# A fused two-block kernel: more of the state space scan beside the expert layers, less beside the attention

## The chip, the cores and the metric

The kernel runs on one core of one Trainium2 chip. The metric is the time of one execution in microseconds (us). The engines of the core are named as in the profile: PE is TensorE (matrix products; PEld its weight loads), DVE is VectorE, ACT is ScalarE, POOL is GpSimd, SP is SyncE. Each engine works through its own list of instructions in order; all five lists run side by side, and an instruction waits until the data and buffers that it needs are ready.

## The reference, cut to what matters

Two blocks follow each other on 8 sequences of 512 tokens with 128 features, all in float32. Each block computes `x = x + s * silu(f)` from the same normalised input.

```
block 0:  s = mamba(xn) -> rms norm -> MLP -> rms norm
          f = two-layer mixture of experts: 24 experts, top 2, four groups of tokens, at most 86 rows
              per expert and group: layer 1 (128 -> 512), layer norm + relu, layer 2 (512 -> 128)
block 1:  s = causal attention, 8 heads of 128
          f = mixture of 128 experts, top 2, at most 32 rows each
mamba:    h[t] = dA[t] * h[t-1] + dBx[t];  y[t] = sum over 16 states of h[t] * C[t]
```

The recurrence runs over 512 tokens, for 256 channels and 16 states, in each of the 8 sequences. The mamba branch and the mixture of block 0 do not depend on each other until the end of the block. The attention of block 1 works sequence by sequence, so it can begin with sequence 0 while the scan still works on the later ones.

## The kernel before, in words

The scan is cut into 64 **steps**. One step handles two of the 16 states of one sequence, so a sequence has 8 steps, and the sequences follow each other; step number n belongs to sequence n // 8, at place k = n % 8. A generator, `model()`, yields after each step, and `step()` runs it one step further. What a step issues (`scan`, L588 to L628):

- ACT issues two DMAs of 512 KB that broadcast two rows of B (`bb`) and of C (`cb`) over the partitions.
- For each half of the channels: ACT makes two tiles `da` (L601); DVE multiplies `bb` into `u` (L603), runs two scans on it (L605) and multiplies `cb` into it (L606). DVE thus does 8 instructions in a step.
- PE transposes `u` and sums it over the states into the bank `py` with 16 matrix products (L627).

Besides the scan, certain places k carry other work of the branch. At k = 0 the sequence before is gated (L647), `py` is opened anew (L616), and the first part of `back` runs (L667 to L678); at k = 1 and k = 2 its second and third parts (L655 to L701, the MLP). At k = 4 and k = 5 the two parts of `front` of the next sequence run (convolution L559, projection L564, then the step size L576 to L584). At k = 6 the gate is computed (L639).

The buffers of the scan are few: two each of `bb`, `cb` and `da`, four of `u`, one of `py`.

The rest of the kernel is written in a fixed order, and the steps are put between its parts by counting. The stages are:

1. Preparation and routing of the 24-expert mixture, then `step()` once.
2. **First layer**: a loop over the 24 experts (`expert1`: POOL gathers token rows, PE transposes and multiplies, ACT scales, SP stores to DRAM).
3. **Joining stage** (`between`): 16 pairs of token tiles are gathered, layer-normalised on DVE and ACT, and stored.
4. **Second layer**: a loop over the 24 experts (`expert2`: gather, four transposes, four products per tile, and so on).
5. **Turn** to block 1: the mixture's result of sequence 0 is gathered and the attention prepared, with 4 steps placed between.
6. **Attention**: 48 heads (8 of each of the sequences 0 to 5), and after each head the share of the steps that are left. Each head's instructions are `probabilities` (L846 to L860) and `values` (L874 to L892); the copy at L876 may go to DVE or ACT.
7. **Last stage**: the last two sequences' heads beside the 128-expert mixture and the output.

A generator `mixture()` runs the stages 2 to 4 and says, after each expert or pair, how many steps that stage should have in all and in how many parts; the caller adds the shares up and calls `step()` whenever more than half a step is due:

```
    for n, of in mixture():
        due += n / of
        while due > 0.5:
            step()
            due -= 1.0
```

The attention takes what is left: `left = NSTEP - taken`, spread evenly over the 48 heads. Place in the code gives priority: the framework that builds the kernel orders each engine's list by it, and lets a later instruction go first where an earlier one would not be ready. So a step need not run exactly where the code has it.

Of the kernel before, what the change touches and what calls it, by code (L numbers as in the profile page):

```python
# [27 lines left out]
E0, C0, DH, H0 = 24, 86, 512, 4  # L28
# [19 lines left out]
def tile_kernel(ctx: ExitStack, tc: tile.TileContext, t: dict, out: bass.AP):  # L48
# [373 lines left out]
    def weights(shape, source):  # L422

        tiles = {}

        def get(e):
            for n in range(e, min(e + 3, E0)):
                if n not in tiles:
                    tiles[n] = me.tile(list(shape), F32, name="we", tag="we", bufs=4)
                    Q.dma_start(tiles[n], source[n])  # L430
            return tiles[e]

        return get

    def expert1(e, w):

        we = w(e)
        px = ps_e.tile([P, SLOTS], F32, name="px", tag="pe")
        for c, r in enumerate(SROWS):
            xg = me.tile([CP, D], F32, name="xg", bufs=8)  # L440
            gather(xg[:r], xn_dram, inv[:r, c, e : e + 1])
            T.transpose(px[:, c * CP : c * CP + r], xg[:r], ident[:r, :r])  # L442
        xT = me.tile([P, SLOTS], F32, name="xTe", tag="xTe")
        S.copy(xT, px)
        hs = me.tile([CP, SG, DH], F32, name="hs", tag="big", bufs=4)
        for c, r in enumerate(SROWS):
            ph = ps_e.tile([CP, DH], F32, name="ph", tag="pe")
            T.matmul(ph[:r], chosen(e, r), bias[:, 0:DH], start=True, stop=False)
            T.matmul(ph[:r], xT[:, c * CP : c * CP + r], we, start=False, stop=True)  # L449
            S.activation(hs[:r, c, :], ph[:r], AF.Copy, scale=wsl[:r, c, e : e + 1])  # L450
        store(hs_dram, e, hs)
# [52 lines left out]
    def expert2(e, w):  # L504
        we = w(e)
        po = ps_e.tile([CP, SG, D], F32, name="po", tag="pe")
        os = me.tile([CP, SG, D], F32, name="os", tag="o")
        hg = me.tile([CP, SG, DH], F32, name="hg", tag="big", bufs=4)
        for c, r in enumerate(SROWS):
            gather(hg[:r, c, :], hid_dram, inv[:r, c, e : e + 1])  # L510
            pt = ps_e.tile([P, NJ, CP], F32, name="pht", tag="pe")
            for f in range(NJ):
                T.transpose(pt[:, f, :r], hg[:r, c, f * P : (f + 1) * P], ident[:r, :r])  # L513
            hT = me.tile([P, NJ, CP], F32, name="hgT", tag="xTe")
            S.activation(hT[:, :, :r], pt[:, :, :r], AF.Relu)  # L515
            T.matmul(po[:r, c, :], chosen(e, r), bias[:, DH:], start=True, stop=False)
            for f in range(NJ):
                T.matmul(po[:r, c, :], hT[:, f, :r], we[:, f, :], start=False, stop=(f == NJ - 1))  # L518
            S.activation(os[:r, c, :], po[:r, c, :], AF.Copy, scale=wsl[:r, c, e : e + 1])
        store(os_dram, e, os)  # L520
# [526 lines left out]
    def mixture():  # L1047
        w = weights((P, DH), t["W1"])
        for e in range(E0):
            expert1(e, w)  # L1050
            yield 11, E0
        w = weights((P, NJ, D), t["W2"])
        w(0)
        for _ in between():
            yield 6, NTT // 2
        for e in range(E0):
            expert2(e, w)
            yield 14, E0

    step()  # L1060
    due = 0.0
# [5 lines that stand above are left out]
# [155 lines left out]
```

## Time and profile before

| | us |
|---|---|
| median of 8 runs | 1605.14 |
| lowest, highest run | 1598.34, 1609.62 |
| time of the profiled execution | 1606.63 |
| its span, first to last instruction | 1604.9 |

| engine | busy us | share of the span |
|---|---|---|
| PE | 1230.3 | 77% |
| DVE | 1244.0 | 78% |
| ACT | 977.4 | 61% |
| POOL | 599.6 | 37% |

The profile is of one execution. Busy time is the union of an engine's instructions; a window view cuts the span into stretches and gives it for each. In the views, `u<-da,u` means an instruction that writes tile `u` and reads `da` and `u`; `x256` is a count; "idle before" is the time in which the engine stood still just ahead of the instructions of a group, with what ended most of it. The median of the runs and the profiled execution differ by 1.5 us.

### The profile page before, as it was taken

What the parts mean: (1) busy time and instruction counts of PE and PEld (TensorE: products, weight loads), DVE (VectorE), ACT (ScalarE), POOL (GpSimd) and SP (SyncE); (2) the same over time, 40 slices, a digit from 0 to 9 for tenths busy, and PEclk for the clock granted to TensorE, in tenths of its full rate; (3) what the DMA queues carried; (4) which work ended last, traced back from release to release, by engine and by line L of the source; (5) the groups of instructions that cost most, each with busy time, mean ns of one, the idle gap of its engine ahead of it and who ended that gap; (6) DMA issues with size and microseconds to landing.
All of it is one profiled execution on the core that took longest, in us unless ns stands there. A gap on an engine that the chain in (4) does not pass through costs nothing.

```text
span 1604.9 us, 20658 instructions
## 1 busy us (share of the span) xinstructions
PE 1230.3 (77%) x6825; PEld 865.8 (54%) x6825; DVE 1244.0 (78%) x2758; ACT 977.4 (61%) x1727; POOL 599.6 (37%) x502
## 2 busy tenths in 40 slices
PE   6778889513379888646889889989889898899763
PEld 4444355313267777523556656766557576567542
DVE  5628775788946858868999999999899996465454
ACT  6035858666747677445776858676587674642452
POOL 1235643556245434473603550043150402010465
PEclk9678989756679999767989999999999999999886
DMA  6267767787467765533222332123122210548143
GB/s 190 77 219 233 250 235 229 228 253 252 165 191 232 236 181 190 146 72 105 62 72 86 79 96 77 53 87 91 59 66 64 82 44 14 139 117 225 50 112 95
DMA packets 170669, 218.84 MB, mean 136 GB/s; under 512 B 16618, under 2 KB 118074, under 8 KB 170562
## 3 DMA queue, kind: packets, MB, share of 16 engines
q1 hardware_dynamic: 126018, 99.39, 20.1%
q10 hardware_dynamic: 18432, 67.12, 12.8%
q0 software_dynamic: 26112, 51.01, 12.2%
q8 instruction: 54, 0.88, 0.2%
q14 instruction: 53, 0.43, 0.1%
HBM read 161.56 MB, written 55.84 MB: 135 GB/s over the span
## 4 chain that ended last, share of the span: by engine, by line
DVE 37%; PE 30%; issue 9%; DMA 8%; POOL 7%; ACT 7%; another core or an unknown queue 2%; SPq 1%; POOLq 0%; DVEq 0%; ACTq 0%
DVE u L605 11%; DVE u L606 5%; PE po L881 4%; PE sc L854 3%; DVE u L603 3%; DVE sc L856 3%; POOL o L131 3%; PE py L627 3%; PE ph L449 2%; PE pp L874 2%; PE po L518 2%; DVE s L892 2%; POOL hd L128 2%; PE pqm L846 2%
## 5 line engine op out<-in xcount | busy, mean ns | idle before, releaser
L605 DVE TENSOR_TENSOR_SCAN u<-da,u 128x512 f32<-128x512 f32 x256 | 312.8, 1243 | 62.8 <-ACT da L601 54.6
L627 PE MATMUL py<-ident,u 128*128 128x128 f32 x1024 | 165.3, 303 | 135.3 <-DVE u L606 135.2
L627 PEld LDWEIGHTS py<-ident,u 128*128 128x128 f32 x1024 | 133.3, 157 | 187.9 <-DVE u L606 169.5
L881 PE MATMUL po<-v,pT 128*128 128x129 f32 x1280 | 185.6, 288 | 29.4 <-DVE pT L876 13.6
L881 PEld LDWEIGHTS po<-v,pT 128*128 128x128 f32 x1280 | 167.6, 200 | 59.8 <-issue 25.0
L601 ACT ACTIVATE da<-dt,a_neg 128x512 f32<-128x512 f32 x256 | 176.2, 718 | 36.1 <-DVE u L605 30.0
L860 ACT ACTIVATE prob<-sc,mn 128x128 f32<-128x128 f32 (+3 forms) x256 | 130.0, 527 | 102.3 <-DVE mn L856 81.2
L854 PE MATMUL sc<-xaT,qm 128*128 128x128 f32 (+3 forms) x512 | 179.5, 460 | 16.7 <-ACT prob L860 14.2
L603 DVE TENSOR_TENSOR u<-bb,lp 128x1024 f32<-128x1024 f32 x128 | 154.8, 1230 | 14.1 <-DMA bb<-xd_dram 11.7
L606 DVE TENSOR_TENSOR u<-u,cb 128x1024 f32<-128x1024 f32 x128 | 157.9, 1233 | 1.2 <-DMA cb<-xd_dram 0.2
L856 DVE CUSTOM_DVE_ANT_0 sc<-sc,mask 128x128 f32<-128x128 f32 (+3 forms) x256 | 124.8, 499 | 39.8 <-PE sc L854 19.9
L131 POOL DMA_INDIRECT o<-os_dram,row x64 | 113.9, 1780 | 79.4 <-DMA bb<-xd_dram 31.7
L874 PE MATMUL pp<-ident,prob 128*128 128x128 f32 x640 | 113.5, 287 | 37.0 <-DVE pT L876 22.5
L128 POOL DMA_INDIRECT xg<-xn_dram,inv x72 | 93.0, 1292 | 120.9 <-PE px L442 59.9
L828 POOL DMA_INDIRECT xs_dram<-xn,idx x64 | 76.4, 1194 | 161.9 <-DVE row L825 73.3
L874 PEld LDWEIGHTS pp<-ident,prob 128*128 128x128 f32 x640 | 80.7, 147 | 96.7 <-issue 32.6
L128 POOL DMA_INDIRECT hg<-hid_dram,inv x72 | 90.8, 1261 | 101.1 <-PE pht L513 72.0
L854 PEld LDWEIGHTS sc<-xaT,qm 128*128 128x128 f32 x512 | 83.6, 197 | 59.9 <-ACT prob L860 30.5
L128 POOL DMA_INDIRECT hd<-hs_dram,row x64 | 82.0, 1281 | 65.3 <-ACT xs L560 23.4
L876 ACT COPY pT<-pp 128x384 f32<-128x384 f32 (+1 forms) x100 | 51.4, 514 | 63.1 <-PE pp L874 60.6
L518 PEld LDWEIGHTS po<-we,hgT 128*128 128x128 f32 (+1 forms) x576 | 71.8, 189 | 23.0 <-issue 18.4
L518 PE MATMUL po<-we,hgT 128*128 128x128 f32 (+1 forms) x576 | 80.5, 287 | 0.9 <-ACT hgT L515 0.8
(289 smaller groups left out, 2567.4 us busy)
## 6 DMA issues: line engine op xcount, KB each, us to landing
bb<-xd_dram ACTq DMA_DIRECT2D x64, 512.0 KB
cb<-xd_dram ACTq DMA_DIRECT2D x64, 512.0 KB
we<-in_W SPq DMA_DIRECT2D x48, 256.0 KB
hs_dram<-hs SPq DMA_DIRECT2D x24, 512.0 KB
hid_dram<-hd SPq DMA_DIRECT2D x32, 256.0 KB
we<-in_we SPq DMA_DIRECT2D x16, 512.0 KB
hs_dram<-hs SPq DMA_DIRECT2D x24, 192.0 KB
xb<-in_x SPq DMA_DIRECT2D x16, 256.0 KB
```

The source lines that it names most:

```text
L128: G.indirect_dma_start(dst, None, table[:, :], IOA(idx, 0))
L131: G.indirect_dma_start(dst, None, table[:, :], IOA(idx, 0), compute_op=ALU.add)
L518: T.matmul(po[:r, c, :], hT[:, f, :r], we[:, f, :], start=False, stop=(f == NJ - 1))
L601: S.activation(da[:, j, :], dt[:, hf, :], AF.Exp, scale=a_neg[:, hf, n0 + j : n0 + j + 1])
L603: V.tensor_tensor(u, bb, bc(dx[:, hf : hf + 1, :], (P, NC, L)), ALU.mult)
L605: V.tensor_tensor_scan(u[:, j, :], da[:, j, :], u[:, j, :], 0.0, ALU.mult, ALU.add)
L606: V.tensor_tensor(u, u, cb, ALU.mult)
L627: T.matmul(py[:, i, hf * P : (hf + 1) * P], us[hf][:, j, i * P : (i + 1) * P], ident, is_transpose=True, start=False, stop=(n0 + j == DS - ...
L854: T.matmul(sc[:, :w], qm[:, i * P : w], xaT[:, :w], start=True, stop=True)
L856: V.tensor_tensor_reduce(sc[:, :w], sc[:, :w], mask[:, L - w :], -1.0, FMAX, ALU.add, ALU.min, mn[:, i : i + 1])
L874: T.transpose(pp[:, c, :], prob[i][:, k * P : (k + 1) * P], ident)
L881: T.matmul(po[:, i - i0, :], pT[:, i * (i + 1) // 2 + k, :], v[:, k, hd % 4, :], start=(k == 0), stop=(k == i),)
```

## The change

Two numbers in `mixture()` are changed. Between the experts of the first layer there are 14 steps instead of 11, and between those of the second layer 20 instead of 14. The joining stage keeps 6 and the turn 4. Since the attention takes what is left, 19 steps instead of 28 are spread over its 48 heads. No instruction is added or removed.

```diff
         for e in range(E0):
             expert1(e, w)
-            yield 11, E0
+            yield 14, E0
         w = weights((P, NJ, D), t["W2"])
         w(0)
         for _ in between():
             yield 6, NTT // 2
         for e in range(E0):
             expert2(e, w)
-            yield 14, E0
+            yield 20, E0
```

By the code, the steps of each stage are then:

| stage | steps before | steps after |
|---|---|---|
| before the first layer | 0 | 0 |
| first layer | 1 to 11 | 1 to 14 |
| joining stage | 12 to 17 | 15 to 20 |
| second layer | 18 to 31 | 21 to 40 |
| turn | 32 to 35 | 41 to 44 |
| attention | 36 to 63 | 45 to 63 |

## The prediction

> **What bounds the kernel now.** I first cut the span into its stages. The ends are read from the first and last instructions of the tiles (the gathers `xg`, `hd`, `hg`, `o`). In the window view each row is a stretch, its length, then busy time of PE, PE's loads, DVE, ACT and POOL (counts in brackets), granted clock of PE, DMA share, GB/s.
>
> ```profile
> 95.00:290.00 195.00, 155.65 (x614) 83.39 (x613) 135.88 (x127) 125.02 (x205) 94.95 (x75) 0.93 0.73 240
> 290.00:448.00 158.00, 53.05 (x238) 41.02 (x237) 134.49 (x225) 104.66 (x181) 82.93 (x67) 0.63 0.71 224
> 448.00:660.00 212.00, 179.49 (x1309) 152.28 (x1309) 142.83 (x135) 144.22 (x277) 92.27 (x75) 0.95 0.65 199
> 660.00:753.00 93.00, 48.99 (x217) 34.05 (x215) 72.95 (x141) 41.80 (x76) 53.73 (x33) 0.67 0.40 104
> 753.00:1345.00 592.00, 528.53 (x2896) 368.62 (x2896) 568.78 (x1418) 413.95 (x713) 181.78 (x132) 0.96 0.25 71
> ...
> 480.00:640.00 160.00, 141.79 (x1070) 118.63 (x1069) 117.20 (x110) 120.51 (x227) 74.12 (x57) 0.99 0.69 214
> ```
>
> The rows are first layer, joining stage, second layer, turn, attention, and the inner part of the second layer. In the attention DVE is busy 568.8 of 592 us, 96%, and PE 89%: DVE sets its length. In the two layers PE leads: 80% in the first, 85% in the second and 89% (141.8 of 160) in its inner part, with DVE at 70% and 67%. So the change takes work from a stage where DVE is full and puts it where DVE has room and PE has little.
>
> Second, the costliest groups give the price of a step.
>
> ```profile
> L605 DVE TENSOR_TENSOR_SCAN u<-da,u 128x512 f32<-128x512 f32 x256 | 312.8, 1243 | 62.8 <-ACT da L601 54.6
> L627 PE MATMUL py<-ident,u 128*128 128x128 f32 x1024 | 165.3, 303 | 135.3 <-DVE u L606 135.2
> L603 DVE TENSOR_TENSOR u<-bb,lp 128x1024 f32<-128x1024 f32 x128 | 154.8, 1230 | 14.1 <-DMA bb<-xd_dram 11.7
> L606 DVE TENSOR_TENSOR u<-u,cb 128x1024 f32<-128x1024 f32 x128 | 157.9, 1233 | 1.2 <-DMA cb<-xd_dram 0.2
> ```
>
> DVE needs (312.8 + 154.8 + 157.9) / 64 = 9.8 us for a step, PE 165.3 / 64 = 2.6 us. Each group's idle time shows the chain: PE waits for `u`, DVE for `da`.
>
> Third, the waits in the inner part of the second layer.
>
> ```profile
> POOL hg L128 <- PE pht L513: 64.4, 16, 7.7
> ACT os L519 <- PE po L518: 28.7, 20, 4.2
> ...
> PE py L627 <- DVE u L606: 12.1, 13, 1.9
> ...
> DVE u L605 <- ACT da L601: 9.9, 6, 4.0
> ...
> DVE u L603 <- DMA bb<-xd_dram: 7.6, 5, 2.8
> ```
>
> POOL and ACT wait for PE, so PE paces the experts; but of PE's 18 us idle, 12.1 are waits for a step's `u` in PE's in-order list.
>
> **The change part by part.** No instruction comes or goes; 9 steps change their neighbours. Which steps they are matters, since places k differ. The prices per sequence, from the group rows (busy time of the whole kernel over 8), on PE: k = 0 opens `py` 21.5 / 8 = 2.7 and does `pyz` and `pr` (9.1 + 19.4) / 8 = 3.6; k = 1 `pzt`, `pf`, `pr` (7.9 + 36.6 + 33.8) / 8 = 9.8; k = 4 `pc` and `pd` (66.6 + 17.1) / 8 = 10.4; k = 5 `pv` 2.3; k = 6 `pz` 2.3. On DVE: k = 0 1.9 (L647, L678); k = 1 1.5 and k = 2 2.2 (eight short ones of L659, L657, L699); k = 4 0.7 (L566); k = 5 7.3 (four of L582 at 1.22, L583, L584).
>
> *First layer*, three steps more (12, 13, 14; k = 4, 5, 6): PE 3 x 2.6 + 10.4 + 2.3 + 2.3 = 22.8; DVE 3 x 9.8 + 0.7 + 7.3 = 37.4.
> *Joining stage*, still six, but places 5 and 6 give way to 2 and 3: PE -4.6, DVE 2.2 - 7.3 = -5.1. DVE is busy 85% there; I take -3.
> *Second layer*, 21 to 40 for 18 to 31: six scans, two more of k = 0, one more each of k = 1, 5 and 6: PE 15.6 + 12.6 + 9.8 + 4.6 = 42.6; DVE 58.8 + 3.8 + 1.5 + 7.3 = 71.4.
> *Turn*, k = 1 to 4 for 0 to 3: PE +4.1, DVE -1.2. PE is 53% busy there and covers it; without that cover it would be 4. I take +3.
> *Attention*, without 36 to 44: PE 9 x 2.6 + 2 x 10.4 + 2.3 + 2.3 + 6.3 + 9.8 = 64.9; DVE 9 x 9.8 + 2 x 0.7 + 7.3 + 1.9 + 1.5 + 2.2 = 102.5.
>
> These are sums of records that overlap by some 5% on an engine (in the attention the branch's share and the rest add to more than the 568.8 of the union), so the attention is left with about DVE 569 - 98 = 471 and PE 529 - 61 = 468. **Both engines are then equal**, where DVE was ahead. The length has bounds: at the 96% that DVE reaches now, 471 / 0.96 = 491; at the 89% that PE has now, 468 / 0.89 = 526. I take 512 (about 92% of either), nearer the second since two full engines in step lose more than one: gain 592 - 512 = 80, bounds 66 and 101.
>
> In the layers the added PE work is the least that can be charged if PE had no room, 21 and 40 us after the overlap; the idle 39 and 32 us of PE could take half of it; the most is the whole DVE time one for one, 37 and 71, if the step's chain sets the pace. I take the added PE time at the present share of PE: 21 / 0.85 = 25 (0.85 is between 80% and the 84% of its inner part) and 40 / 0.89 = 45. DVE is then (136 + 36) / 220 = 78% and (143 + 68) / 257 = 82% busy, below the 85% of the joining stage, so it can just follow.
>
> Each moved step also brings its ACT work (four `da` of 0.72 us, 2.9 us, plus its table loads of 1.28 us) and two 512 KB DMAs to queues where an expert's scalings stand. ACT goes from 144 of 212 to about 186 of 257 us, 72%, as in the attention (70%): no term. The DMAs take 3.1 us of all 16 engines per MB (19.7% of 212 us for 13.5 MB); the six steps add 19 us to 138 us busy, but the stage grows too, so the share stays near 0.65: no term. Should the `bb` wait double, that is 8 us, inside the range.
>
> Sum: -80 + 25 + 45 - 3 + 3 = -10 us on the profiled 1606.6. I take a little more, -14: in the rows above the granted clock rises with PE's share (0.63 at 34%, 0.93 at 80%, 0.95 at 85%, 0.99 at 89%), so a denser first layer may come from 0.93 to 0.95, which is 2% of 178 us, 4 us. That gives 1592.6; the median of the runs stands 1.5 us below the profiled time, so 1592 holds for either.
>
> [...] The gathers of the layers last longest beside the scan: `xg` issues take 909 / 966 / 2003 ns (least, median, most), `ya` in the last stage, with no step near, 940 / 944 / 1337. Both layers have 72 gathers with a mean of 1.29 and 1.26 us, so some 0.33 us x 144 = 47 us of POOL are lost now; with DVE 8 to 15 points busier than its present 67 to 70%, some 8 more. POOL idles over 95 us in each layer and waits for PE, so the sum has no term for it. [...]
>
> **The rivals.**
> *Slower: the step's chain sets the pace of the layers.* In the layers DVE has nothing but the scan (all its records there are of the branch), so each wait for `da` (ACT's list stands behind scalings that wait for PE) is lost, and PE then waits for `u`. For it: 26.8 us of waits for `da` in the first layer, and 12.1 of PE for `u`. Then the layers grow by DVE's time, 36 + 68 = 104, and the gain is 80: +24, 1630. It decides once DVE passes about 85% in the second layer. Against it: DVE has nearly no wait in the attention at 96%.
> *No change:* PE stays at 89% in the attention (gain 66) and the layers cost 66 to 70: 1605 to 1610.
> *More gain:* idle time of PE in the layers takes half of what comes, +33, and the attention reaches 96%, -101, or 92%, -80: -47 to -68, 1540 to 1560.
>
> **How the numbers follow.** Forecast (1575 to 1600) 0.38; more gain 0.12; no change 0.10; slower 0.40, as the second layer would have to hold 82% of DVE with a chain that now idles a third of its time. A measurement of this kernel tells about 0.3%, 5 us. Faster 0.50, same 0.10, slower 0.40. The range for 8 in 10 runs from 1562 (part of "more gain") to 1634 (the slower rival with a little over); the likeliest case alone has 1575 to 1600.
>
> **What the next profile would show.** If right: the second layer is 250 to 262 us long, the first 215 to 225, PE's share about 0.85 in both; the attention about 512 us with DVE and PE within 3 points of each other. If the slower rival holds: a second layer over 275 us with DVE over PE and longer waits of DVE for `da` and PE for `u`. If the attention is still over 530 us, my equal-engines figure is wrong; if the layers grow by under 40 us together, PE had room that the busy time hides.

## The result: 4% slower, and the profile after

The changed kernel takes 1671.65 us (median of 16 runs), the kernel before 1605.05 us in the runs beside it (46 runs): ratio 1.040, 95% interval 1.038 to 1.042. The medians differ by 67 us. The profiled execution has a span of 1661.7 us against 1604.9, so 57 us are to be found in the profile.

First the window view of the kernel after, by the same stages as before: first layer, joining stage, second layer, turn, attention, last stage, and then the inner part of the second layer. The columns are the length of the stretch, busy time of PE, PE's loads, DVE, ACT and POOL, granted clock, DMA share, GB/s.

```profile
95.00:314.00 219.00, 170.88 (x665) 90.97 (x663) 157.95 (x146) 139.28 (x222) 93.41 (x75) 0.92 0.68 223
314.00:480.00 166.00, 72.70 (x296) 52.68 (x296) 146.26 (x241) 105.17 (x194) 81.26 (x65) 0.64 0.71 228
480.00:747.00 267.00, 208.96 (x1472) 174.72 (x1472) 203.56 (x194) 175.02 (x326) 93.68 (x77) 0.92 0.59 181
747.00:852.00 105.00, 56.03 (x217) 34.53 (x217) 75.48 (x144) 52.39 (x85) 58.47 (x37) 0.67 0.37 94
852.00:1406.00 554.00, 482.01 (x2619) 340.00 (x2617) 475.39 (x1321) 366.15 (x633) 162.76 (x123) 0.95 0.21 57
1406.00:1661.70 255.70, 194.12 (x1164) 137.10 (x1162) 136.74 (x466) 111.32 (x207) 82.61 (x85) 0.88 0.43 118
500.00:735.00 235.00, 185.64 (x1307) 153.36 (x1306) 179.07 (x173) 158.57 (x296) 78.70 (x62) 0.93 0.59 181
```

The attention lost 38 us (592 to 554), where 80 was forecast. DVE and PE are nearly equal in it, 475 and 482 us, as the prediction said (471 and 468), but each is busy for only 86% and 87% of it. The second layer grew by 55 us, from 212 to 267, and PE's share in it fell from 85% to 78%. The first layer grew by 24, the joining stage by 8 and the turn by 12 in these cuts.

In both layers DVE's idle time hardly changed: 195 - 135.9 = 59 us and 219 - 158.0 = 61 in the first, 212 - 142.8 = 69 and 267 - 203.6 = 63 in the second. The layers grew by about the DVE time that came in, 22 and 61 us.

The steps did not fall quite where the code has them. Counted by the starts of the 256 scans (L605, four to a step; the step ahead of the first layer in the code runs in it):

| steps by the trace | first layer | joining | second layer | turn | attention |
|---|---|---|---|---|---|
| before | 12.75 | 6.25 | 13 | 5.25 | 26.75 |
| after | 14.75 | 7.25 | 19 | 5.75 | 17.25 |

So the first layer got two steps more and not three, and the joining stage got one more.

Second, the four groups of a step, from the costliest groups of the kernel after. After the bar: busy time, mean ns of one, idle time before them and its main releaser.

```profile
L605 DVE TENSOR_TENSOR_SCAN u<-da,u 128x512 f32<-128x512 f32 x256 | 307.7, 1227 | 53.4 <-ACT da L601 40.9
L627 PE MATMUL py<-ident,u 128*128 128x128 f32 x1024 | 169.2, 312 | 141.7 <-DVE u L606 128.5
...
L603 DVE TENSOR_TENSOR u<-bb,lp 128x1024 f32<-128x1024 f32 x128 | 153.0, 1219 | 17.3 <-DMA bb<-xd_dram 17.3
...
L606 DVE TENSOR_TENSOR u<-u,cb 128x1024 f32<-128x1024 f32 x128 | 158.0, 1234 | 1.3
```

Counts and durations are those of before (DVE 1227 for 1243, 1219 for 1230, 1234 for 1233 ns; PE 312 for 303 ns). No step became dearer in itself on DVE: the time went to how the steps fit between the rest.

Third, the waits in the inner part of the second layer (engine, line, what it waited for: total us, times, longest).

```profile
POOL hg L128 <- PE pht L513: 112.9, 17, 14.8
ACT os L519 <- PE po L518: 58.4, 31, 5.3
...
PE py L627 <- DVE u L606: 30.7, 27, 8.2
DVE u L605 <- ACT da L601: 24.1, 10, 6.8
DVE u L603 <- DMA bb<-xd_dram: 12.8, 4, 9.7
```

PE now stands 30.7 us for a step's `u`, in 235 us; before it was 12.1 in 160, which would be 18 in a stretch of this length. For DVE's waits for `da`, 24.1 us, the inner 160 us of before (9.9) are too short a stretch. From 470 to 650 us, before, the two waits are:

```profile
DVE u L605 <- ACT da L601: 19.5, 8, 7.7
...
PE py L627 <- DVE u L606: 14.4, 14, 2.3
```

In 235 us that would be 25 us for `da` and 19 for `u`. So PE's waits for `u` grew, and DVE's waits for `da` did not. The waits suggest a ring: PE's in-order list waits for `u` of DVE, the experts' products behind it wait, ACT's scalings wait for those, and the `da` that ACT has behind its scalings come late to DVE. That the last link of it costs more than before is not shown.

Last, what is new in the attention, from its waits (852 to 1400 us).

```profile
PE pp L874 <- DVE pT L876: 23.5, 9, 12.6
...
DVE xn L117 <- DMA xs_dram<-xn,idx: 18.0, 3, 12.6
...
DVE lno_st L107 <- DMA o<-os_dram,row: 10.1, 5, 5.5
```

The prepared rows `xn2` (the tile behind L117) have one buffer. DVE may not normalise the next sequence into it before POOL's scatters of the sequence before (`xs_dram`, L828) have read it. At 1060 us the scatters stand in POOL's list among the gathers of the next sequence (`o`, L131); DVE stands 12.6 us, and PE, which waits for a copy that DVE makes after it, stands 12.6 us as well. In the attention of before, PE's waits for `pT` are 10.5 us, the longest 3.6, and none of DVE for `xs_dram` shows.

In the tables from here on, the stages run from first gather to first gather, and the attention from its first head to the 49th, so that all kernels are cut alike. Time in us:

| kernel | first layer | joining | second layer | turn | attention | last | span |
|---|---|---|---|---|---|---|---|
| before | 194 | 159 | 215 | 88 | 629 | 225 | 1605 |
| after | 221 | 163 | 270 | 102 | 588 | 221 | 1662 |
| difference | +27 | +4 | +55 | +14 | -41 | -4 | +57 |

(The start, up to the first gather, is 95 and 97 us.)

### The profile page after: what moved, and what is told of

Its sections match the earlier page's. It is cut to its first block, busy times and chain, and to the rows that moved or that the text cites. A ratio compares the mean times of both kernels' runs of the same rounds, so it can differ in the third digit from the quotient of the medians.

```text
span 1661.7 us, 20649 instructions
## 1 busy us (share of the span) xinstructions
PE 1255.6 (76%) x6825; PEld 881.2 (53%) x6825; DVE 1247.8 (75%) x2758; ACT 984.7 (59%) x1732; POOL 585.9 (35%) x502
## 4 chain that ended last, share of the span: by engine, by line
DVE 32%; PE 29%; issue 12%; DMA 9%; POOL 8%; ACT 8%; another core or an unknown queue 1%; SPq 0%; POOLq 0%; ACTq 0%; DVEq 0%
DVE u L605 10%; DVE u L606 5%; PE sc L854 4%; PE po L881 4%; POOL o L131 3%; PE py L627 3%; DVE u L603 3%; DVE sc L856 2%; PE pp L874 2%; PE ph L449 2%; DMA hd<-hs_dram,row 2%; PE po L518 2%; POOL xs_dram L828 2%; PE pqm L846 2%; PE pc L559 1%
## 5 line engine op out<-in xcount | busy, mean ns | idle before, releaser
L605 DVE TENSOR_TENSOR_SCAN u<-da,u 128x512 f32<-128x512 f32 x256 | 307.7, 1227 | 53.4 <-ACT da L601 40.9
L627 PE MATMUL py<-ident,u 128*128 128x128 f32 x1024 | 169.2, 312 | 141.7 <-DVE u L606 128.5
L627 PEld LDWEIGHTS py<-ident,u 128*128 128x128 f32 x1024 | 135.8, 161 | 203.9 <-DVE u L606 169.8
L603 DVE TENSOR_TENSOR u<-bb,lp 128x1024 f32<-128x1024 f32 x128 | 153.0, 1219 | 17.3 <-DMA bb<-xd_dram 17.3
L606 DVE TENSOR_TENSOR u<-u,cb 128x1024 f32<-128x1024 f32 x128 | 158.0, 1234 | 1.3
L128 POOL DMA_INDIRECT hg<-hid_dram,inv x72 | 89.9, 1248 | 159.0 <-PE pht L513 112.9
L128 POOL DMA_INDIRECT xg<-xn_dram,inv x72 | 91.9, 1277 | 147.1 <-PE px L442 86.3
L131 POOL DMA_INDIRECT o<-os_dram,row x64 | 112.3, 1754 | 77.5 <-DMA os_dram<-os 37.4
L828 POOL DMA_INDIRECT xs_dram<-xn,idx x64 | 74.6, 1165 | 128.6 <-DVE idx L822 66.8
L518 PE MATMUL po<-we,hgT 128*128 128x128 f32 (+1 forms) x576 | 84.7, 293 | 3.1 <-ACT hgT L515 3.1
L449 PE MATMUL ph<-we,xTe 128*128 128x512 f32 x144 | 75.7, 643 | 8.8 <-ACT xTe L444 8.8
L518 PEld LDWEIGHTS po<-we,hgT 128*128 128x128 f32 (+1 forms) x576 | 75.1, 196 | 13.3 <-issue 8.1
```

The lines of the kernel that those rows point to most:

```text
L128: G.indirect_dma_start(dst, None, table[:, :], IOA(idx, 0))
L131: G.indirect_dma_start(dst, None, table[:, :], IOA(idx, 0), compute_op=ALU.add)
L603: V.tensor_tensor(u, bb, bc(dx[:, hf : hf + 1, :], (P, NC, L)), ALU.mult)
L605: V.tensor_tensor_scan(u[:, j, :], da[:, j, :], u[:, j, :], 0.0, ALU.mult, ALU.add)
L606: V.tensor_tensor(u, u, cb, ALU.mult)
L627: T.matmul(py[:, i, hf * P : (hf + 1) * P], us[hf][:, j, i * P : (i + 1) * P], ident, is_transpose=True, start=False, stop=(n0 + j == DS - ...
```

## The experiments

Kernels that ran together share the runs of the kernel before. The kernel before took 1577 us on the chip of the first four and 1604 to 1606 on the others, so results are compared as ratios. The last stage of those first four is 206 to 212 us long, that of all others 220 to 227, which is about half of the difference. Where the rest lies is not known, since no profile here shows the kernel before on that chip. A stage of the first four is therefore compared with 629, 588 or 270 only with a doubt of some 12 us.

### Each part alone, and the other way

```diff
-            yield 11, E0     # first layer
-            yield 14, E0     # second layer
+            yield 14, E0  /  yield 14, E0     first part alone
+            yield 11, E0  /  yield 20, E0     second part alone
+            yield  8, E0  /  yield 11, E0     the other way
```

> Only the first layer's number changed (14 steps there, second layer 14 as before, 25 beside the attention). Theory A (in the layers a step's own chain of ACT, DVE and PE sets the price, about 8 us a step; in the attention a step is worth only PE's share of it, 4 to 5 us): first layer +24 us as in the changed kernel, attention -13, total +8 to +20 us, 1613 to 1625. Theory B (the layers' cost is only PE's added work, and the loss is a stall in the attention, where the next sequence's normalisation waits for a scatter): first layer +22, attention -30, total -10 to 0.

> Only the second layer's number changed (20 steps there, first layer 11 as before, 22 beside the attention). Theory A: second layer +50 to +58 us, attention -25, total +25 to +45 us, 1630 to 1650. Theory B: second layer +45, attention -50 to -60 unless the stall is there, total -15 to 0.

> The other direction: 8 steps beside the first layer, 11 beside the second, 34 beside the attention. Theory A: layers -50 us, attention +25 to +35 (its PE work grows by 6 x 5 us, its DVE work by 6 x 11), total -15 to -25, faster than before. Theory B (the attention is bound by DVE, 96% busy): attention +66, layers -40, total +25 us.

| steps: first / joining / second / attention | ratio, 95% | first layer | second layer | turn | attention |
|---|---|---|---|---|---|
| 14 / 6 / 14 / 25 | 1.023 (1.019 to 1.028) | 222 | 203 | 97 | 624 |
| 11 / 6 / 20 / 22 | 1.022 (1.017 to 1.026) | 196 | 272 | 98 | 586 |
| 8 / 6 / 11 / 34 | 1.018 (1.015 to 1.022) | 161 | 194 | 85 | 699 |

Both parts lose by themselves, and their losses add up to about the whole. The other way loses as well: six steps more in the attention make it 70 us longer, while the layers win 33 and 21. Of the divisions tried, that of before is the best. Against the expectations: the first part alone lost 35 us by the medians, more than either theory had; the second lost 36, as theory A had it; and the other way lost 27, where theory A had a gain and theory B, with the attention bound by DVE, had +25 and +66 for the attention.

A step in the attention has no single price. On the chip of these three, 34, 25 and 22 steps give 699, 624 and 586 us, that is 8.3 and then 12.7 us for a step, about DVE's 9.8. On the others, 28 and 19 give 629 and 588, 4.6 us for a step. Each of these kernels also has its own order, and chips differ: in the first one the second layer, with its 14 steps of before, is 12 us shorter than in the kernel before. So these differences are not exact prices.

### The stall in the attention

```diff
-            xn2 = at.tile([P, NJ, D], F32, name="xn2", bufs=1)
+            xn2 = at.tile([P, NJ, D], F32, name="xn2", bufs=2)
```

> The changed kernel with two buffers instead of one for the normalised input of the attention, which the scatters on POOL's queue read. Theory B (the stall in the attention is the loss): the 12.6 us wait of DVE for the scatter goes and the attention is 25 to 40 us shorter than the changed kernel's 554 us, total 1630 to 1645. Theory A: the wait goes but the time lands in PE's other waits; 5 to 15 us at most, total 1655 to 1667.

Ratio to before 1.029 (1.026 to 1.032), on the changed kernel. That is 1.1% better than the changed kernel. DVE's wait for `xs_dram` is gone, and the attention is 576 us for 588; but this is one of the four runs on the faster chip, and the joining stage and the second layer, which the edit does not touch, are 4 and 8 us shorter too. The stand of both engines did not go either. It came at another place, where DVE waits for the gather of `o`:

```profile
DVE lno_st L107 <- DMA o<-os_dram,row: 10.3, 2, 8.4
...
PE pp L874 <- DVE ln_rs L111: 7.8, 1, 7.8
```

So what the stall was worth is not shown. In the window view of this kernel the attention reads:

```profile
840.00:1415.00 575.00, 509.53 (x2763) 354.33 (x2761) 486.18 (x1351) 382.16 (x677) 171.63 (x133) 0.95 0.20 56
```

PE's share is 509.5 / 575 = 88.6%, that of before (559.1 / 629 = 88.9%). A second try at the same stall moved the preparation of the next sequence to other heads (fetch, joining and preparation after heads 0, 4 and 5 instead of 1, 3 and 4):

```diff
-                if hd == 1:
+                if hd == 0:
                     got = fetch(b + 1)
-                if hd == 3:
+                if hd == 4:
                     xb = after(b + 1, *got)
-                if hd == 4:
+                if hd == 5:
                     ready[b + 1] = beside.prepare(b + 1, xb)
```

> The changed kernel with the gather of the next sequence one head earlier and its norm and preparation one head later in the attention (heads 0, 4, 5 instead of 1, 3, 4). If DVE's waits in the attention for the gathered `o` and for the scatter are what keeps the gain small: they fall from 28 us to under 8 and the attention from 588 to 560 to 568, ratio 1.022 to 1.030. If PE's pace is: 580 to 590, ratio 1.035 to 1.042.

Ratio 1.032 (1.029 to 1.034), so 0.8% better than the changed kernel; but the attention is 586 us for 588, and the gain stands in the second layer (262 for 270), which the edit does not touch. In the attention (846 to 1432 us) DVE's waits for the scatter fell from 18.0 to 5.8 us, the longest from 12.6 to 3.2, and yet PE stands 11.8 us at one place:

```profile
PE pp L874 <- DVE pT L876: 15.3, 8, 11.8
DVE lno_st L107 <- DMA o<-os_dram,row: 11.3, 4, 7.9
```

Here most of the scatter's wait went and the attention gained 2 us, as the expectation had it for PE's pace. The stall by itself is thus not shown to be worth its 12.6 us.

### Less work of one engine: first with the order free, then with the order fixed

To ask which engine binds a stage I made its work lighter. The multiplication by `cb` (L606) covers 32 of 512 columns, so part of the output is left out; or half of the transposes of L627 are left out.

```diff
-                V.tensor_tensor(u, u, cb, ALU.mult)
+                nl = 32 if 36 <= b * DS // NC + n0 // NC <= 63 else L
+                V.tensor_tensor(u[:, :, 0:nl], u[:, :, 0:nl], cb[:, :, 0:nl], ALU.mult)
```

```diff
-                    for i in range(NJ):
+                    for i in range(2 if 36 <= b * DS // NC + n0 // NC <= 63 and n0 + NC < DS else NJ):
```

(the same with 21 to 40 for the second layer)

> The kernel before, with the last multiplication of a step (u by cb, L606) cut to 32 of 512 columns in steps 36 to 63, those beside the attention: 2.3 us of DVE less in each of 28 steps, 64 us, PE and ACT unchanged (part of the result is left out). If DVE bounds the attention, as the prediction had it, the attention shrinks by 50 to 60 us. If PE paces it through its own list and the waits in it, by 5 to 20 us.

> The kernel before, with half of a step's transposes (L627) left out in steps 36 to 63 (but in the last of each sequence): 8 of 16 products in 25 steps, 1.2 us each, 30 us of PE less, DVE unchanged (part of the sum is left out). If DVE bounds the attention, it shrinks by 0 to 8 us; if PE paces it, by 25 to 35 us.

> The changed kernel, with L606 cut to 32 of 512 columns in steps 21 to 40, those beside the second layer: 2.3 us of DVE less in each of 20 steps, 46 us. If the step's chain on DVE sets the pace of the second layer, it goes from 267 to 270 us to about 225 to 235. If PE does, to 255 to 265.

> The changed kernel, with half of a step's transposes left out in steps 21 to 40 (but in the last of each sequence): 18 steps by 1.2 us, 22 us of PE less. If the step's chain on DVE sets the pace of the second layer, it stays within 5 us; if PE does, it shrinks by 20 to 26 us.

| edit | ratio, 95% | its stage was | its stage is |
|---|---|---|---|
| before, lighter DVE in the attention | 1.026 (1.023 to 1.029) | 629 | 669 |
| before, lighter PE in the attention | 1.009 (1.004 to 1.014) | 629 | 641 |
| after, lighter DVE in the second layer | 1.037 (1.034 to 1.040) | 270 | 264 |
| after, lighter PE in the second layer | 1.036 (1.028 to 1.045) | 270 | 270 |

Less work made the attention longer. No theory of a bound gives that. The framework orders each engine's list from its own estimates of durations, so a shorter instruction moves others, and the test had changed two things at once. I therefore built each kernel twice: the first build records every engine's list and the engine chosen for each free copy; the second has the lighter instructions and is tied to the recorded lists.

```diff
+    for run in ORDER["runs"]:                    # one list for each engine
+        for a, b in zip(run, run[1:]):
+            tc.add_manual_dep(traced[b], traced[a].name, ..., reason="order")
...
-                V.tensor_tensor(u, u, cb, ALU.mult)
+                nl = 32 if LIGHT[0] and 36 <= b * DS // NC + n0 // NC else L
+                V.tensor_tensor(u[:, :, 0:nl], u[:, :, 0:nl], cb[:, :, 0:nl], ALU.mult)
```

For PE each transpose is kept, but takes 32 rows of `u` and writes 32 columns:

```diff
-     py[:, i, hf * P : (hf + 1) * P], us[hf][:, j, i * P : (i + 1) * P], ident,
+     py[:, i, hf * P : hf * P + nl], us[hf][0:nl, j, i * P : (i + 1) * P], ident[0:nl, 0:nl],
```

> The kernel before with every engine's list in its own order, instruction by instruction, and L606 cut to 32 of 512 columns in steps 36 to 63 (part of the result is left out): 64 us of DVE less. If DVE bounds the attention, the stretch from its first head to the last stage's first head goes from 629 to 570 to 585 us, total 1550 to 1565. If PE and the waits between the lists do, to 605 to 625, total 1585 to 1602.

> The same fixed order of the kernel before, the transposes of steps 36 to 63 shortened from 128 to 32 columns (part of the sum is left out): 40 to 50 us of PE less, DVE unchanged. If DVE bounds the attention: 0 to 10 us shorter, total 1595 to 1605. If PE does: 35 to 45 us shorter, total 1560 to 1570.

> The changed kernel's order on every engine, L606 cut to 32 columns in steps 21 to 40: 46 us of DVE less beside the second layer and the joining stage's end. If the step's DVE work sets the pace there, the second layer goes from 270 to 230 to 240 us. If PE's work or the lists' waits on PE do, 255 to 268.

> The changed kernel's order on every engine, the transposes of steps 21 to 40 shortened to 32 columns: 30 to 36 us of PE less. If the step's DVE work sets the pace of the second layer: 262 to 270. If PE's work does: 235 to 245.

| edit, order fixed | ratio, 95% | its stage was | its stage is |
|---|---|---|---|
| before, lighter DVE in the attention | 0.982 (0.978 to 0.987) | 629 | 608 |
| before, lighter PE in the attention | 1.007 (1.004 to 1.010) | 629 | 644 |
| after, lighter DVE in the second layer | 1.024 (1.020 to 1.028) | 270 | 247 |
| after, lighter PE in the second layer | 1.040 (1.035 to 1.045) | 270 | 275 |

Three readings. First, the attention in the window view: before, then with lighter DVE and the order fixed, then with the order free.

```profile
751.00:1380.00 629.00, 559.05 (x3042) 387.98 (x3041) 582.73 (x1465) 432.08 (x754) 189.70 (x140) 0.96 0.24 68
```
```profile
747.00:1355.00 608.00, 552.18 (x3041) 384.44 (x3040) 534.26 (x1464) 431.02 (x754) 185.98 (x140) 0.97 0.24 70
```
```profile
750.00:1419.00 669.00, 571.06 (x3042) 395.69 (x3040) 543.03 (x1473) 434.04 (x750) 177.88 (x140) 0.94 0.22 65
```

With the order kept, 48 us less DVE work shortened the stage by 21, that is 0.43 for one. DVE then fills 88% and PE 552 / 608 = 91%: PE was close behind DVE all along. The third row has the same instructions in another order and is 61 us longer (PE is busy 19 us more in it, at a clock of 0.94 for 0.97). So the order alone, which nobody wrote, is worth 61 us here, as much as the whole change. The 608 us lie in the range expected if PE and the waits between the lists pace the stage (605 to 625).

Second, the second layer of the changed kernel with lighter DVE and fixed order, and then three of its waits from 500 to 720 us (its line numbers are 12 or 13 higher: L617 is the scan, L640 the transposes).

```profile
480.00:723.00 243.00, 208.15 (x1494) 176.84 (x1495) 171.11 (x197) 175.13 (x328) 78.69 (x75) 0.93 0.63 200
```
```profile
DVE u L617 <- ACT da L613: 24.4, 11, 4.9
PEld py L640 <- DVE u L619: 16.2, 13, 6.8
...
PE py L640 <- DVE u L619: 12.7, 10, 6.6
```

DVE has 32 us less, PE the same 208; the layer is 23 us shorter and PE's share is back at 208 / 243 = 86%. PE's waits for `u` went from 30.7 us (in 235) to 12.7 (in 220), while DVE's for `da` stayed (24.1 and 24.4). So DVE's chain inside a step, not PE's work, holds these 23 us, although DVE was only 76% busy. The 247 us lie between the two expected ranges (230 to 240, 255 to 268): most of DVE's time counts, not all.

Third, the lighter products did not take time off PE as a whole: the clock was lower with them (0.93 for 0.96 in the attention, 0.82 for 0.92 in the second layer; see the last section), and products that the edit does not touch took longer, in the second layer 323 ns for 292 (L530, L518 in the changed kernel, beside the run with lighter DVE in the same order). PE's busy time rose, with the order kept and DVE's work the same. The attention with them:

```profile
752.00:1396.00 644.00, 571.62 (x3041) 385.37 (x3040) 582.70 (x1461) 432.61 (x754) 186.12 (x140) 0.93 0.24 66
```

So these two runs can be read as tests of a slower PE. In the attention 12.5 us more of PE (571.6 for 559.1) made the stage 15 us longer; in the second layer 17 us more (226.1 for 209.0) made it 5 us longer. With one profiled execution each the figures are rough, but they fit the first two readings: in the attention PE's time counts, in the second layer DVE's.

### Taking the waits out of a step

If PE's in-order list stands for `u`, the transposes may be issued one step later; if DVE stands for `da`, the four `da` may be single tiles, each free as soon as its scan is done.

```diff
+            held.append((n0, us))
+            while held and (len(held) > 1 or n0 + NC == DS):
+                m0, hu = held.pop(0)
...                              # the transposes of L627, with hu and m0
-                da = ms.tile([P, NC, L], F32, name="da")
+                das = [ms.tile([P, L], F32, name="da", bufs=4) for j in range(NC)]
```

> The changed kernel with a step's transposes (L627) issued one step later in the code, so that PE meets them only when `u` should long be there. Theory C (in the layers each step costs a round of waits between the engines' lists, above all PE standing before `u`: 30.7 us in the second layer): the waits of PE for `u` there fall below 12 us, the second layer from 270 to 240 to 250 and the first from 221 to 205 to 212, total 30 to 45 us less than the changed kernel, ratio to before 1.010 to 1.020. Theory D (the order that the framework finds is the cause and any new order costs about the same): second layer 260 to 275, ratio 1.03 to 1.045.

> The changed kernel with `da` held as four single tiles instead of two double ones: the same memory, but ACT can begin a tile as soon as one scan has read one. Theory C: the waits of DVE for `da` in the second layer fall from 24 us to about 10, the second layer from 270 to 255 to 262, ratio 1.03 to 1.035. Theory D: no such shift, second layer 262 to 275, ratio 1.035 to 1.045.

> The kernel before with the transposes issued one step later. Theory C: PE's waits for `u` go here too (14.4 us in the inner part of the second layer, 17 in the first): layers 15 to 25 us shorter, ratio 0.985 to 0.992. Theory D: a new order, and the kernel before is a good one: ratio 1.01 to 1.03.

| edit | ratio, 95% | first layer | joining | second layer | turn | attention |
|---|---|---|---|---|---|---|
| after, transposes one step later | 1.019 (1.017 to 1.022) | 214 | 157 | 264 | 93 | 588 |
| after, single `da` | 1.028 (1.025 to 1.030) | 223 | 165 | 267 | 102 | 578 |
| before, transposes one step later | 1.004 (1.002 to 1.006) | 191 | 153 | 205 | 93 | 644 |

Transposes one step later give the changed kernel half of its loss back (1.040 to 1.019): 28 us in the four stages ahead of the attention. Yet PE still stands for `u`, as the waits from 500 to 715 us show (L631 is here the transposes, L606 the scan; the stretch has 215 us, that of the changed kernel had 235):

```profile
POOL hg L128 <- PE pht L513: 83.2, 18, 10.8
ACT os L519 <- PE po L518: 46.4, 32, 3.7
PEld py L631 <- DVE u L607: 36.3, 19, 9.2
PE py L631 <- DVE u L607: 31.9, 18, 9.1
DVE u L606 <- ACT da L602: 17.3, 9, 6.8
```

The wait was not removed, 31.9 us for 30.7; perhaps a step of distance is not enough when the steps come close together. What went down is what the experts wait for: POOL 112.9 to 83.2, ACT 58.4 to 46.4, DVE for `da` 24.1 to 17.3. The edit was made to take PE's wait away; the gain is real, but it did not come by that way. Single `da` gave 1.2%, 10 us of it in the attention and 3 in the second layer; but the waits for `da` that it was to take away (500 to 735 us) are 24.4 us for 24.1, so this gain did not come by its way either. On the kernel before, the later transposes did halve PE's waits for `u` (7.0 us from 470 to 640, for 14.4 from 470 to 650). They made the stages ahead of the attention 14 us shorter and the attention 15 us longer, and the ratio fits neither theory.

The last two runs put these cures together on the division of before (single `da` and two buffers of `xn2`; the second with the later transposes too).

> The kernel before (11, 14, 28) with the decays da as four single tiles and with two buffers for the second normalization's rows (xn2). On the changed kernel each of the two gave 1.1 to 1.2% in earlier runs. If they take away waits that every division of the steps has, the kernel before gains too: 0.985 to 0.995. If what they gave there was mostly another order of the instructions, made by chance, the kernel before, whose order is a good one, loses with a new one: 1.00 to 1.02.

> The same with the transposes of u issued one step later, so that TensorE does not stand for u inside a step. On the changed kernel this gave 33 us, on the kernel before 13 to 19 us in the layers and as much lost in the attention. If the ring of waits inside a step is what a step costs beside the layers: 0.98 to 1.00. If the order decides: 1.00 to 1.02, with the loss in the attention again.

| before with | ratio, 95% | first layer | joining | second layer | turn | attention |
|---|---|---|---|---|---|---|
| single `da`, two `xn2` | 1.006 (1.002 to 1.009) | 196 | 157 | 212 | 87 | 640 |
| and later transposes | 0.998 (0.995 to 1.000) | 191 | 154 | 208 | 91 | 641 |

Edits that gave 1.1 and 1.2% on the changed kernel cost 0.6% here, by 11 us in the attention, though they only loosen waits; the likely reason is the new order. The last one wins 12 us ahead of the attention and loses as much in it. It is the fastest complete version of all, by 4 us, while the runs of the kernel before beside it differ by 16 us among themselves (1594.75 to 1610.98).

## Why the prediction was wrong, by its own steps

| term | forecast | measured (table of stages) |
|---|---|---|
| attention | -80 | -41 |
| first layer | +25 | +27 |
| second layer | +45 | +55 |
| joining stage | -3 | +4 |
| turn | +3 | +14 |
| clock, first layer | -4 | none (0.93 to 0.92) |
| start, last stage | 0 | -2 |
| sum | -14 | +57 |

**The step that failed** is the length of the attention: "I take 512 (about 92% of either)", gain 80. Its 39 us are over half of the 71 by which the sum was off. In its own cut it came to 554, and the 42 us between can be laid out. PE's work fell to 482 and not 468; at the forecast's share of 468 / 512 = 91.4%, that is 527, or 15 us. PE's share did not rise above the 89.3% of before: 482 / 0.893 = 540, another 13. The last 14, by which the share fell to 87%, are not settled: the new stall has this size, but the run in which most of its wait went gained 2 us. The prediction took DVE's 96% as the bound of the stage and let PE's share rise from 89% to 91.4% once DVE had room. The fixed-order runs show the error: 48 us off DVE alone gave 21, with PE then at 91%, and 12.5 us more of PE cost 15. PE did not pass 91% of this stage in any run here. The prediction's worst case for the gain, 66, took PE's 89% with the forecast's 468 us; with the work that PE really had it would have been 52.

Why PE had 14 us more work can be seen for the most part: the prices, taken as means over the whole kernel, were too high for the attention. The transposes of L627 fell there by 18.4 us (62.9 to 44.4) where 23.4 were taken off, the products of L559 and L564 by 19.0 for 20.8, those of the MLP (L689, L694) by 6.4 for 8.8. The 5% for overlap was also too little: the groups' rows of this stage add up to some 623 us on PE where the engine is busy 529.

**First layer: right in size by luck** (+24 in its own cut, +25 forecast). By the trace two steps came in and not three, and PE's added work was 15 and not 21 us; at the forecast's share of 0.85 that is 18 us. What the layer did grow by is DVE's added time, 22 us, the case that the prediction had as its most. The two errors cancel.

**Second layer: the term was too small by 10.** PE's work grew by 29.5 us and not by 40; at the forecast's share of 0.89 that would have been 33 us. The measured 55 are nearer to DVE's added 61 us, with DVE's idle time as before (63 us for 69). The sentence that failed is "DVE is then (...) 82% busy (...) so it can just follow". DVE was only 76% busy and could not follow; with 32 us less on DVE the 85% share came back and 23 us with it. A share of busy time does not tell how long a chain through two engines takes. The prediction's 186 us of ACT do not follow from its prices either (144 + 6 x 4.2 = 169, measured 175), but no term rested on them.

**Turn and joining stage** were put at +3 and -3. The joining stage got a step more by the trace, and DVE's busy time in it rose by 11.8 us where a fall of 5.1 was forecast. The turn's work grew little (DVE 73.0 to 75.5, PE 49.0 to 56.0 us), but PE's waits for `u` in it are 26.4 us for 12.7 before. That a step between the short DVE instructions ahead of the first head delays them is likely, but was not tested by itself. The later transposes brought the turn back to 93 us and the joining stage to 157.

**The rivals.** The slower one was right in direction and in its mechanism for the layers: the step's chain sets the pace, and they grow by DVE's time (it gave them 104 us; DVE's added time was 83, and they took 82). It was wrong in its condition: it was to decide "once DVE passes about 85%", and it decided at 76%. Its sign, a second layer over 275 us with longer waits for `da`, did not come. And it took the same 80 us for the attention, so its 1630 fell short of 1671 too. The "no change" rival had PE's share in the attention (89%) nearly right and the layers' cost too small. The "more gain" rival was the opposite of what happened.

**The gathers** have no place in the sum after the fact either. The prediction put some 47 us of POOL down as lost beside the scan, and some 8 more for a busier DVE. In the trace of before the gathers of the two layers do last longer beside DVE: 39 of the 144 have no DVE instruction at their side and take 0.95 us on average in the first layer and 0.94 in the second, the other 105 take 1.44 and 1.36. Why they do is not shown by any run. But the 8 us did not come: with eight steps more beside it by the trace, POOL's busy time in the two layers went from 95.0 to 93.4 and from 92.3 to 93.7 us, and the mean gather from 1.29 to 1.28 and from 1.26 to 1.25 us. What POOL's gathers wait for in the layers is above all PE (86.3 us for `px`, 112.9 for `pht` in the kernel after).

**The signs that the prediction named** did their work: "If the attention is still over 530 us, my equal-engines figure is wrong" came true at 554. It got the two engines' equal times right, and this did not help; what it got wrong was the share that both could reach.

**What stays open.** How much of the 57 us is the moved work, and how much is only a worse order, can't be told apart, since moving a step is itself a change of order. That order weighs as much is shown (61 us in the attention, 17 in the second layer, 264 free against 247 fixed, for the same instructions). That the change loses by more than chance of order is likely, as both parts alone lose 2% and nearly add up, but it was shown for these orders only. The two cures of the changed kernel were not run together on it.

## What to carry to other kernels

Before moving work off the fullest engine, ask what the second fullest can reach there: here DVE at 96% hid a PE at 89%, and PE never passed 91%, so 48 us off DVE were worth 21. Work that is a chain through several engines can cost the stage that receives it more than its share of the busiest engine: eight steps more (by the trace) cost 82 us in the layers, 10 us each, about DVE's whole time for them, though neither engine was over 80% busy. And where a framework orders the lists, an experiment that changes an instruction's size changes the order too: fix the order, or the result measures both.

## What the runs showed of the hardware that was not expected

In the second layer the granted clock of TensorE fell from 0.92 to 0.82 when a step's transposes were made narrower, with the order and the number of instructions unchanged. First the attention, where this is less clear: the window view of 760 to 1300 us, before and with narrower transposes in fixed order.

```profile
760.00:1300.00 540.00, 478.06 (x2610) 333.16 (x2611) 518.45 (x1281) 381.44 (x659) 171.32 (x124) 0.96 0.27 75
```
```profile
760.00:1300.00 540.00, 476.35 (x2527) 319.13 (x2527) 507.30 (x1239) 370.35 (x634) 168.60 (x123) 0.92 0.27 74
```

Then the second layer of the changed kernel with narrower transposes:

```profile
480.00:752.00 272.00, 226.11 (x1498) 188.03 (x1498) 207.38 (x197) 177.69 (x330) 87.71 (x76) 0.82 0.57 178
```

In the attention the clock is 0.92 for 0.96 at the same PE busy time, but other kernels with products of full width have 0.94 to 0.97 over the attention, so this alone shows little. In the second layer it is 0.82 for 0.92, where PE was busier (226 of 272 us, 83%, against 78%); the run beside it with the same order and products of full width has 0.93. PE's total rose in both (571.6 for 559.1 us in the whole attention), so narrower transposes did not make either stage shorter. The prediction had taken the clock to rise with PE's share, and between the stages of the kernel before it does (0.63 at 34% busy, 0.67 at 53%, 0.93 at 80%, 0.95 at 85%, 0.96 at 89%); across these two kernels it does not (0.92 at 78%, 0.82 at 83%). What sets the clock was not tried further.
